# Moving the work around layer 1's attention: PSUM banks for its first chains, another DMA queue for its input, and a softmax sum on TensorE

## The chip, the core and the metric

The kernel runs on one core of one Trainium2 chip. A core has five engines that work beside one another and wait for each other through semaphores: TensorE (PE, matrix products, with its weight loads shown as PEld), VectorE (DVE), ScalarE (ACT), GpSimd (POOL) and SyncE (SP), which here only issues DMA transfers. TensorE writes its results into PSUM, which has eight banks of 128 x 512 f32; the other operands lie in SBUF. The metric is the device time of the program in microseconds, given as the median of several runs.

## What is computed

The input x is 4 x 1024 x 512 in f32. Two layers follow, each of the form

```
xn = layernorm(x)
x  = x + attention(xn) * silu(feed_forward(xn))
```

Layer 0 has a linear attention with decay and a feed-forward with ternary weights and an exact gelu. Layer 1, where the change lies, has softmax attention with 16 heads of width 32 and a rotation of half of each head (rope), and a gated feed-forward with integer weights:

```
q, k, v = xn @ wq.T, xn @ wk.T, xn @ wv.T        (16 heads of 32)
q, k    = rope(q), rope(k)
p       = softmax(q k^T / sqrt(32))
s       = (p v) @ wo.T
```

## The kernel before

The 4096 rows are 32 tiles of 128 (t), or 8 blocks of 512. Layer 0's attention comes first, then its feed-forward, then layer 1's attention, then its feed-forward. TensorE's order is the order of the program; the other engines' instructions are put in order by a planner ahead of the run, from its own costs, and each engine then works strictly in that order. An instruction marked `keep_in_program_order` may not be moved ahead of what the program issues before it on its engine; later ones may still pass it in the planning.

**The end of layer 0.** `gate` (L646) finishes one tile of x after layer 0: y = projection plus a correction (L658, reads PSUM), tanh on ScalarE (L660), two VectorE passes (L661, L662), the addition of the old x on POOL (L663), a store of the tile to DRAM as x1 through SP's queue (L664), and the tile's moments (L105, L108). The last block's four tiles (28 to 31) are finished while layer 1 starts.

**The start of layer 1's attention.** PSUM is now split into `ring` (three tiles of two banks), `acc1` (one bank) and `y` (one bank). `heads_in` (L884) makes k, q and v of four heads of one batch element as six chains of matmuls: k half 0, k half 1, q half 0, q half 1, v half 0, v half 1 (halves of the 1024 tokens). A k or q chain ends with `raw`, a ScalarE copy (L905); eight small transfers on SP (L909) that bring each row's rotation partner into `rr`; the product with the cosines on VectorE (L912, reads PSUM); the product with the sines and the sum on POOL (L913, L914). There is one `rr` tile for half 0 and one for half 1, so k and q of a half use it in turn, and two `raw` tiles. The first six chains run alone (L1077); `spread` (L979) gives them a bank of `ring` and `acc1` alternately.

`rr` and the tiles for the maxima (`m2`) are set to zero on VectorE (L847, L850).

**Late tiles.** The last four tiles of x1 weren't normalised in layer 0. `late` (L862) reads each back from DRAM through SP (L866) and normalises it on ScalarE (L869, kept in program order; one buffer for x, one for the result); two steps afterwards `late_turn` (L873) transposes it on TensorE into `acc1`. Steps 0, 4, 8, 12 load, steps 2, 6, 10, 14 transpose.

**The main loop** (L1084) runs over steps s. A unit is 512 queries of one batch element and one group of four heads: 32 units of 8 steps. In step s TensorE computes scores for the row maxima of unit s // 8 (`top`: sq in two ring tiles, reduced by VectorE, L1004), scores with keys on the partitions ten steps behind (`expo`: sk in two ring tiles, the maximum subtracted by L1033, then the exponential p on ScalarE, L1038), and p times v another step behind (`weigh`: y). After a unit's eight steps `turn_max` (L1006) transposes its maxima through `acc1`; ScalarE copies them (mf, mh) and VectorE makes mT (L1016), which L1033 needs. Between these, `advance` runs a piece of a chain of the next four heads, or of the output projection `wo`, in `acc1`.

The softmax denominators: POOL adds the eight p tiles of a unit into `part` (L1065, L1067), and one group of matmuls with ones (`total`, L940) sums over the partitions into z; `divide` (L945) takes reciprocals on VectorE and multiplies on POOL. Only for the last unit (31) TensorE sums the first four p itself (z_last). In the last ten steps, and for what belongs to them, VectorE does the additions in POOL's place. During the last twelve steps with sq, weights for the feed-forward are loaded and converted on VectorE (L783).

Of the kernel before, what the change touches and what calls it, by code (L numbers as in the profile page):

```python
# [16 lines left out]
ALU = mybir.AluOpType  # L17
# [3 lines left out]
B, N, D = 4, 1024, 512  # L21
# [6 lines left out]
NBLK = NT // BLK  # L28
# [7 lines left out]
def kernel(ctx, tc, ins, out):  # L36
    nc = tc.nc
# [21 lines left out]
    x1_t = x1.rearrange("(t p) d -> t p d", p=P)  # L59
# [486 lines left out]
    with ExitStack() as es:  # L546
# [99 lines left out]
        def gate(blk, i):  # L646

            t = blk * TPB + i
            mv = mvs[blk]

            last = blk == NBLK - 1 and i >= 2
            x = p2.tile([P, D], F32, tag="x" if last else "xr", name=f"x0r_{t}")
            nc.sync.dma_start(out=x, in_=x_t[t])
            s = p2.tile([P, D], F32, tag="xq" if last else "s", name=f"s0_{t}")
            nc.sync.dma_start(out=s, in_=s0_t[t])
            sc = mv[:, 3, i : i + 1]
            y = p2.tile([P, D], F32, tag="y", name=f"y0_{t}")
            nc.vector.scalar_tensor_tensor(y, rows, mv[:, 0, i : i + 1], ds.pop(i), ALU.mult, ALU.add)  # L658
            th = x1s[t] = p2.tile([P, D], F32, tag="th", name=f"th0_{t}", bufs=5)
            nc.scalar.activation(th, y, AF.Tanh, scale=sc)  # L660
            nc.vector.scalar_tensor_tensor(th, th, 1.0, y, ALU.add, ALU.mult)  # L661
            nc.vector.scalar_tensor_tensor(th, th, sc, s, ALU.mult, ALU.mult)  # L662
            nc.gpsimd.tensor_tensor(th, th, x, ALU.add)  # L663
            nc.sync.dma_start(out=x1_t[t], in_=th)  # L664
            moments(p2, th, st1[:, t, :], f"c{t}")

        def turn_out(blk, i):
# [139 lines left out]
    with ExitStack() as es:  # L807
# [6 lines left out]
        def ring(name):  # L814
            return pp.tile([P, 2, 512], F32, tag="ring", name=name, bufs=3)

        def acc1(name):
            return pp.tile([P, 512], F32, tag="acc1", name=name)

        TB = N // P  # L820
# [23 lines left out]
        partner = []  # L844
        for i in range(2):
            m2 = wp.tile([P, TPB, P], F32, tag=f"m2_{i}", name=f"m2_{i}")
            nc.vector.memset(m2, 0.0)  # L847
            twice.append(m2)
            rr = wp.tile([P, 512], F32, tag=f"rr_{i}", name=f"rr_{i}")
            nc.vector.memset(rr, 0.0)  # L850
            partner.append(rr)

        def cols4(out, lhsT, rhs, start, stop):
# [8 lines left out]
        def late(i):  # L862

            t = NTILE - TPB + i
            x = p2.tile([P, D], F32, tag="x", name=f"x1_{t}", bufs=1)
            nc.sync.dma_start(out=x, in_=x1_t[t])  # L866
            xn = p2.tile([P, D], F32, tag="xn", name=f"xn1_{t}", bufs=1)
            tc.keep_in_program_order(
                nc.scalar.activation(  # L869
                    xn, x, AF.Identity, bias=shift[:, t : t + 1], scale=st1[:, t, 1:2]  # L870
                )
            )
            return xn  # L873
# [131 lines left out]

        def turn_max(u):  # L1006

            tp = acc1(f"tr_m_{u}")
            for i in range(TPB):
                nc.tensor.transpose(tp[:, i * P : (i + 1) * P], twice[u % 2][:, i, :], ident)  # L1010
            mf = p2.tile([P, 512], F32, tag="mf", name=f"mf_{u}", bufs=1)
            nc.scalar.copy(mf, tp)
            mh = p2.tile([P, 512], F32R, tag="mh", name=f"mh_{u}", bufs=1)
            nc.scalar.copy(mh, mf)
            mTs[u] = p2.tile([P, 512], F32R, tag="mT", name=f"mT_{u}")
            nc.vector.scalar_tensor_tensor(  # L1016
                mTs[u], mh.bitcast(F32), second, mf, ALU.mult, ALU.add
            )
# [34 lines left out]
        def exps(e):  # L1053
            if not 0 <= e < TB * nu:
                return
            u, kb = divmod(e, TB)
            pT = pTs[e] = p2.tile([P, 4, 512], F32, tag="pT", name=f"pT_{e}", bufs=3)
            expo(u, kb, pT)


            k0 = TB // 2 if u == nu - 1 else 0
            add = nc.vector if e + LAG >= TB * nu else nc.gpsimd
            if kb == k0 + 1:
                parts[u] = p2.tile([P, 4, 512], F32, tag="part", name=f"part_{u}")
                add.tensor_tensor(parts[u], pTs[e - 1], pT, ALU.add)  # L1065
            elif kb > k0:
                add.tensor_tensor(parts[u], parts[u], pT, ALU.add)  # L1067
# [6 lines left out]
        nu, LAG = len(units), TB + 2  # L1074
        yTs = {b: {} for b in range(B)}
        chain = None
        for m, c in enumerate(heads_in(0, 0, spread)):  # L1077
            chain = c
            advance(8)
            if m == 3:  # L1080
                norm1(NBLK - 1, p2)
        must, spare = deque(), deque()
        mx, mTs, pTs, ys, parts, lates, soon = {}, {}, {}, {}, {}, {}, {}
        for s in range(TB * nu + LAG + 1):  # L1084

            e = s - LAG
            if s % (2 * TB) == 0 and s < TB * nu:  # L1090

                assert not must
                n = s // (2 * TB) + 1
                if n < 4 * B:
                    b, g = divmod(n, 4)
                    must.extend(heads_in(b, g, acc1))
                    if g == 3 and b + 1 < B:
                        load1(b + 1)
                left = 2
            if s in soon and s < TB * nu:  # L1100
                spare.extend(wo_out(*soon.pop(s), acc1))
            if s % 2 == 0:

                chain = None
                if spare and left and s < TB * nu:
                    chain = spare.popleft()
                    left -= 1
                elif must:
                    chain = must.popleft()
            if s == 2 * TB:  # L1110
                W["wo"] = shared_tile("wo", "wo")
                tc.keep_in_program_order(
                    nc.sync.dma_start(
                        out=W["wo"], in_=ins["woT"].rearrange("(k p) n -> p k n", p=P)
                    )
                )
            if s % 4 == 0 and s // 4 < TPB:
                lates[s + 2] = s // 4, late(s // 4)
            if s < TB * nu:
                u, j = divmod(s, TB)  # L1120
                if j == 0:
                    mx[u] = p2.tile([P, TPB, 4, 2], F32, tag="mx", name=f"mx_{u}")
                for pair in range(2):
                    top(u, j, pair, mx[u])
                if j == TB - 1:
                    m2 = twice[u % 2].rearrange("p q (h c) -> p q h c", c=HD)
                    for c in range(2):
                        nc.vector.tensor_reduce(m2[:, :, :, c], mx[u], AX.X, ALU.max, negate=True)
                    del mx[u]
            late_exp = s >= TB * nu  # L1130
            if late_exp:
                exps(e)
            if 1 <= e <= TB * nu:
                u, kb = divmod(e - 1, TB)
                if kb == 0:
                    ys[u] = pp.tile([P, 512], F32, tag="y", name=f"y_{u}")
                weigh(u, kb, pTs[e - 1], ys[u])
                if u == nu - 1:

                    if kb == 0:  # L1140
                        z_last = acc1("z_last")
                    if kb < TB // 2:
                        total(z_last, pTs[e - 1], kb, TB)
                pTs.pop(e - 2, None)
                if kb == TB - 1:
                    yr = p2.tile([P, 512], F32, tag="yr", name=f"yr_{u}", bufs=1)
                    nc.scalar.copy(yr, ys[u])
                    ys[u] = yr
            held = 0
            zu = (s - (6 if s >= TB * nu else 4)) // TB - 2  # L1150
            if s % TB == 0 and 0 < s <= TB * nu:
                turn_max(s // TB - 1)
            elif s % TB == (6 if s >= TB * nu else 4) and 0 <= zu < nu - 1:
                z = ring(f"z_{zu}")[:, 0, :] if s >= TB * nu else acc1(f"z_{zu}")
                total(z, parts.pop(zu), 0, 1)
                divide(units[zu], ys.pop(zu), z)
                b, g, qh = units[zu]
                if g == 3:
                    soon[s + 4] = b, qh, yTs[b]
            elif s in lates:  # L1160
                late_turn(*lates.pop(s))
            else:
                held = 1
                advance(1)
            if not late_exp:
                exps(e)
            advance(4 - held)
            if TB * nu - 12 <= s < TB * nu:

                nxt = weight(raw1, w0, True)  # L1170
                if loaded:
                    loaded()
                loaded = nxt
                if s == TB * nu - 1:
                    loaded()
# [310 lines left out]
```

## Time and profile before

| what | value |
|---|---|
| median of 3 runs | 3150.0 us (3148.52 to 3150.66) |
| the profiled execution | 3149.29 us, span 3147.5 us |
| TensorE busy | 3088.4 us, 98% |
| VectorE, ScalarE, POOL busy | 1905.1, 1196.1, 1501.4 us |
| mean granted TensorE clock | 0.994 |
| layer 0's last projection ends | about 1164.2 us |
| layer 1's first score matmul | 1198.15 us |
| layer 1's output projections start after the loop | about 2628.4 us |
| layer 1's feed-forward starts | 2657.81 us |

Times in the profile are microseconds from the start of the span; L909 is line 909 of the kernel. A line of the waits names who waited, for whom, the total, how often, and the longest. A line of the chain of waits gives the start, the length, the engine and the line. A line of the timeline gives the start, the length, the engine, the line and what it reads and writes; matmuls of one kind in succession are merged with their number. "SPq" is SP's DMA queue. Busy time of TensorE includes short stalls between pipelined matmuls, so a busy engine isn't always at full speed.

### The profile page before, as it was taken

What the parts mean: (1) busy time and instruction counts of PE and PEld (TensorE: products, weight loads), DVE (VectorE), ACT (ScalarE), POOL (GpSimd) and SP (SyncE); (2) the same over time, 40 slices, a digit from 0 to 9 for tenths busy, and PEclk for the clock granted to TensorE, in tenths of its full rate; (3) what the DMA queues carried; (4) which work ended last, traced back from release to release, by engine and by line L of the source; (5) the groups of instructions that cost most, each with busy time, mean ns of one, the idle gap of its engine ahead of it and who ended that gap; (6) DMA issues with size and microseconds to landing.
All of it is one profiled execution on the core that took longest, in us unless ns stands there. A gap on an engine that the chain in (4) does not pass through costs nothing.

```text
span 3147.5 us, 61092 instructions
## 1 busy us (share of the span) xinstructions
PE 3088.4 (98%) x26233; PEld 1765.4 (56%) x26233; DVE 1905.1 (61%) x2638; ACT 1196.1 (38%) x1696; POOL 1501.4 (48%) x615
## 2 busy tenths in 40 slices
PE   9999999999999998999999999999999999999998
PEld 5555555578777874443344444334444435888887
DVE  4444555468888775656656555555555684566655
ACT  3111111155555542444444444444444444333332
POOL 0000000034444344898888988888888970000001
PEclk9999999999999999999999999999999999999999
DMA  3111111122222231100001000010000013322211
GB/s 131 54 54 54 54 57 44 38 64 91 81 81 71 94 138 38 48 9 8 8 17 40 12 12 15 20 35 14 10 17 15 12 44 100 119 75 66 67 51 55
DMA packets 97799, 158.46 MB, mean 50 GB/s; under 512 B 13040, under 2 KB 26864, under 8 KB 97392
## 3 DMA queue, kind: packets, MB, share of 16 engines
q1 hardware_dynamic: 96704, 151.33, 15.5%
q8 instruction: 207, 3.39, 0.5%
q0 software_dynamic: 816, 3.15, 0.3%
q14 instruction: 72, 0.59, 0.1%
HBM read 104.10 MB, written 41.94 MB: 46 GB/s over the span
## 4 chain that ended last, share of the span: by engine, by line
PE 84%; DVE 11%; issue 2%; ACT 2%; POOL 1%; SPq 1%; DMA 0%; ACTq 0%; POOLq 0%; DVEq 0%
PE sk L1027 9%; PE sq L1000 8%; PE y L1046 8%; PE qk L350 7%; PE gate L1218 5%; PE up L1218 5%; PE dn L1240 5%; PE v1ps L856 4%; PE v0ps L324 3%; PE wo L333 3%; PE wo L856 3%; PE wq L856 3%; PE fc L588 3%; PE wk L856 3%; PE pj L641 3%; PE sk L1033 2%
## 5 line engine op out<-in xcount | busy, mean ns | idle before, releaser
L1067 POOL TENSOR_TENSOR part<-part,pT 128x2048 f32<-128x2048 f32 x184 | 844.8, 4591 | 25.7 <-ACT pT L1038 16.5
L1004 DVE TENSOR_REDUCE mx<-sq 128x2 f32<-128x1024 f32 x512 | 603.3, 1218 | 384.3 <-PE sq L1000 383.1
L1038 ACT ACTIVATE pT<-sk 128x1024 f32<-128x1024 f32 x512 | 496.3, 1021 | 619.4 <-PE sk L1033 616.1
L1027 PE MATMUL sk<-wqT,wkT 32*128 32x512 f32 x2048 | 332.5, 645 | 4.3 <-DVE mx L1004 4.3
L1000 PE MATMUL sq<-wkT,wqT 32*128 32x512 f32 x2048 | 322.5, 641 | 6.1 <-ACT pT L1038 5.1
L1046 PE MATMUL y<-pT,v 128*32 128x512 f32 x2048 | 276.3, 610 | 0.2 <-ACT pT L1038 0.2
L609 POOL TENSOR_TENSOR sums<-sums,h 128x512 f32<-128x512 f32 x112 | 162.9, 1455 | 228.9 <-ACT h L593 223.8
L641 PE MATMUL pj<-wpj,hp 128*128 128x512 f32 x1024 | 265.2, 397 | 5.8 <-DVE hp L601 4.9
L588 PE MATMUL fc<-xp,wfc 128*128 128x512 f32 x1024 | 261.1, 397 | 2.9 <-ACT h L593 2.0
L1262 POOL TENSOR_TENSOR th<-th,x 128x512 f32<-128x512 f32 x31 | 40.1, 1295 | 457.9 <-DVE th L1261 377.0
L1033 PE MATMUL sk<-mT,onesr 2*128 2x512 f32 x1024 | 239.3, 788 | 2.2 <-DVE mT L1016 2.2
L357 POOL TENSOR_TENSOR qd<-qT,wqkv 128x512 f32<-128x512 f32 x32 | 41.1, 1285 | 405.0 <-ACT qT L355 379.1
L350 PE MATMUL qk<-xnT,wqkv 128*128 128x512 f32 x512 | 230.0, 602 | 0.7 <-ACT xnT L148 0.7
L641 PEld LDWEIGHTS pj<-wpj,hp 128*128 128x128 f32 x1024 | 190.0, 188 | 58.2 <-DVE hp L601 17.4
L588 PEld LDWEIGHTS fc<-xp,wfc 128*128 128x128 f32 x1024 | 187.3, 188 | 44.4 <-ACT h L593 5.0
L1027 PEld LDWEIGHTS sk<-wqT,wkT 32*128 32x128 f32 x2048 | 99.9, 184 | 138.0 <-issue 111.4
L1218 PE MATMUL gate<-xp,wf 128*128 128x512 f32 x704 | 174.1, 389 | 0.0
L1065 POOL TENSOR_TENSOR part<-pT,pT 128x2048 f32<-128x2048 f32 x31 | 141.2, 4555 | 69.0 <-ACT pT L1038 68.8
L1218 PE MATMUL up<-xp,wf 128*128 128x512 f32 x704 | 173.8, 389 | 0.0
L1240 PE MATMUL dn<-wf,hp 128*128 128x512 f32 x704 | 173.5, 389 | 0.0
L601 DVE TENSOR_TENSOR hp<-h,hp 128x512 fp32r<-128x512 f32 x128 | 116.9, 913 | 76.2 <-ACT hp L598 76.1
L350 PEld LDWEIGHTS qk<-xnT,wqkv 128*128 128x128 f32 x512 | 95.2, 191 | 112.8 <-issue 104.2
(219 smaller groups left out, 4543.4 us busy)
## 6 DMA issues: line engine op xcount, KB each, us to landing
s<-s SPq DMA_DIRECT2D x96, 256.0 KB
x<-x SPq DMA_DIRECT2D x36, 256.0 KB
x<-in_x SPq DMA_DIRECT2D x32, 256.0 KB
raw_fc<-in_w_fcT SPq DMA_DIRECT2D x32, 256.0 KB
x0f<-in_x SPq DMA_DIRECT2D x32, 256.0 KB
x0r<-in_x SPq DMA_DIRECT2D x32, 256.0 KB
x<-th SPq DMA_DIRECT2D x32, 256.0 KB
xnT<-xnT_d SPq DMA_DIRECT2D x8, 1024.0 KB
```

The source lines that it names most:

```text
L350: nc.tensor.matmul(a, lhsT=wqkv[k][:, c0 : c0 + P], rhs=xnTs[blk][:, k, :], start=(k == 0), stop=(k == KD - 1),)
L588: nc.tensor.matmul(a, lhsT=wfc[k][:, c * P : (c + 1) * P], rhs=xp[n][:, k, :].bitcast(F32R), start=(k == 0 and n == 0), stop=(k == KD - 1 ...
L641: nc.tensor.matmul(ds[i], lhsT=hparts[blk, c][n][:, i * P : (i + 1) * P], rhs=wpj[c], start=(c == 0 and n == 0), stop=(c == NH0 - 1 and n ...
L856: nc.tensor.matmul(out[r0 : r0 + HD, :], lhsT=lhsT[:, r0 : r0 + HD], rhs=rhs, start=start, stop=stop,)
L1000: nc.tensor.matmul(sq[:, hh, :], lhsT=qT[r, q0 : q0 + P], rhs=kT[r, n * 512 : (n + 1) * 512], start=True, stop=True,)
L1004: nc.vector.tensor_reduce(mx[:, qt, 2 * pair : 2 * pair + 2, n], sq, AX.X, ALU.max)
L1027: nc.tensor.matmul(sks[h // 2][:, h % 2, :], lhsT=kT[r, kb * P : (kb + 1) * P], rhs=qT[r, qh * 512 : (qh + 1) * 512], start=True, stop=False,)
L1038: nc.scalar.activation(pT[:, 2 * pair : 2 * pair + 2, :], sks[pair], AF.Exp, scale=QKS)
L1046: nc.tensor.matmul(y[r, :], lhsT=v[:, kb, r], rhs=pT[:, h, :], start=(kb == 0), stop=(kb == TB - 1),)
L1067: add.tensor_tensor(parts[u], parts[u], pT, ALU.add)
L1218: nc.tensor.matmul(a, lhsT=ws[n, c][:, k, :], rhs=xp[m][:, k, :], start=(k == 0 and m == 0), stop=(k == KD - 1 and m == 1),)
L1240: nc.tensor.matmul(ds[i], lhsT=hparts[blk, c][n][:, i * P : (i + 1) * P], rhs=w, start=(c == 0 and n == 0), stop=(c == NH1 - 1 and n == 1),)
```

## The change

It has three parts.

1. In `gate`, for the last block only, the addition of x goes from POOL to VectorE and the store of x1 from SP's queue to POOL's. The four clearing passes of `m2` and `rr` go from VectorE to POOL. The loads in `late` are kept in program order.
2. The first six chains of layer 1 take the six banks of the three ring tiles, one each, in place of `spread`.
3. For unit 30 (`nu - 2`) the additions into `part` are left out, and `total` runs on each p tile as it comes, eight groups of matmuls into `acc1`. Its `divide` comes with its last y. Since `acc1` is taken meanwhile, unit 29's z and unit 31's transposed maxima go to a ring tile. Step 6 as the late time of z is gone.

```diff
-            nc.gpsimd.tensor_tensor(th, th, x, ALU.add)
-            nc.sync.dma_start(out=x1_t[t], in_=th)
+            add, queue = (nc.vector, nc.gpsimd) if blk == NBLK - 1 else (nc.gpsimd, nc.sync)
+            add.tensor_tensor(th, th, x, ALU.add)
+            queue.dma_start(out=x1_t[t], in_=th)
...
-            nc.vector.memset(m2, 0.0)
+            nc.gpsimd.memset(m2, 0.0)
...
-            nc.vector.memset(rr, 0.0)
+            nc.gpsimd.memset(rr, 0.0)
...
-            nc.sync.dma_start(out=x, in_=x1_t[t])
+            tc.keep_in_program_order(nc.sync.dma_start(out=x, in_=x1_t[t]))
...
-            tp = acc1(f"tr_m_{u}")
+            tp = ring(f"tr_m_{u}")[:, 0, :] if u == nu - 1 else acc1(f"tr_m_{u}")
...
+            if u == nu - 2:
+                return
...
-        for m, c in enumerate(heads_in(0, 0, spread)):
+        firsts = [ring(f"first_{i}") for i in range(3)]
+        firsts = [firsts[i][:, n, :] for i, n in ((0, 0), (0, 1), (1, 1), (1, 0), (2, 1), (2, 0))]
+        for m, c in enumerate(heads_in(0, 0, lambda name: firsts.pop(0))):
...
-                if u == nu - 1:
+                if u >= nu - 2:
                     if kb == 0:
-                        z_last = acc1("z_last")
-                    if kb < TB // 2:
+                        z_last = acc1(f"z_{u}")
+                    if u < nu - 1 or kb < TB // 2:
                         total(z_last, pTs[e - 1], kb, TB)
...
+                    if u == nu - 2:
+                        divide(units[u], ys.pop(u), z_last)
+                        soon[s] = units[u][0], units[u][2], yTs[B - 1]
...
-            zu = (s - (6 if s >= TB * nu else 4)) // TB - 2
+            zu = (s - 4) // TB - 2
...
-            elif s % TB == (6 if s >= TB * nu else 4) and 0 <= zu < nu - 1:
-                z = ring(f"z_{zu}")[:, 0, :] if s >= TB * nu else acc1(f"z_{zu}")
+            elif s % TB == 4 and 0 <= zu < nu - 2:
+                z = ring(f"z_{zu}")[:, 0, :] if zu == nu - 3 else acc1(f"z_{zu}")
```

## The prediction, made before the changed kernel was run

> **What bounds the kernel now.** I read the page first: TensorE against the other engines, and its clock.
>
> ```profile
> PE 3088.4 (98%) x26233; PEld 1765.4 (56%) x26233; DVE 1905.1 (61%) x2638; ACT 1196.1 (38%) x1696; POOL 1501.4 (48%) x615
> ...
> PEclk9999999999999999999999999999999999999999
> ```
>
> TensorE is busy for 98% of the span. Time can be won only where it waits (59 us of 3147.5), or where its clock is low, which tenths of forty slices hide. So the list of waits on PE comes next, and it points to the seam before layer 1 and to the end of its attention.
>
> ```profile
> PE v1ps L856 <- DVE wqT L912: 5.8, 1, 5.8
> ...
> PE wk L856 <- DVE y L658: 2.3, 1, 2.3
> PE sk L1033 <- DVE mT L1016: 2.2, 1, 2.2
> ```
>
> These are single waits. The first two, and one of 1.24 before chain 4, are for the one PSUM bank (acc1) that chains 2, 4 and 6 of the first six share. The chain of waits tells more: through the seam it runs over SP, not over a bank.
>
> ```profile
> 1174.94 1.29 POOL th L663
> 1177.16 0.81 SPq L909
> ...
> 1193.24 2.02 DMA rr<-raw_wq
> 1195.48 1.27 POOL rr L913
> 1196.83 1.28 POOL wqT L914
> 1198.15 1.01 PE sq L1000 x5
> ```
>
> The first score matmul (sq, 1198.15) waits for the rotated q: eight small partner copies each for k half 0, k half 1 and q half 0, 24 issues of about 0.67 us one after the other on SP, then a landing of 2 us and two POOL passes of 1.27. They begin at 1177.16 only because SP holds the four x1 stores and the first late load ahead of them; their data was there at 1171.24 (ScalarE's copy raw_wk, 1170.65 + 0.59). Last, the clock by stretches of time (columns: stretch, length, busy PE, PEld, DVE, ACT, POOL, granted clock, DMA share, GB/s):
>
> ```profile
> 1191.40:1194.00 2.60, 2.60 (x52) 2.40 (x56) 2.37 (x9) 0.00 (x0) 1.21 (x1) 0.50 0.18 35
> 1194.00:1198.00 4.00, 3.77 (x84) 3.27 (x76) 0.66 (x5) 0.15 (x1) 2.44 (x2) 0.63 0.13 24
> ...
> 2600.00:2603.00 3.00, 1.43 (x13) 0.36 (x14) 3.00 (x3) 0.84 (x1) 0.00 (x0) 1.00 0.00 0
> 2603.00:2606.00 3.00, 3.00 (x20) 1.62 (x20) 0.72 (x1) 2.20 (x4) 0.00 (x0) 0.54 0.00 0
> ```
>
> After the gap of 5.8 the clock is half; a 64-matmul chain that takes 3.66 us in the timeline takes 6.40. After the 2.24 us wait at 2601.57 it is half again.
>
> **The change, part 1: banks and SP queue.** With six banks the chains run back to back: 1164.10 + 6 x 3.65 = 1186.0, instead of ending at 1197.77. But the sq matmul does not follow the chains, it follows SP. From the first partner copy to sq took 1198.15 - 1177.16 = 21.0, and nothing in that stretch is changed. The x1 stores go to POOL, the first late load is pinned behind the copies, so the first copy follows raw_wk. Earliest: the first chain ends at 1167.76, plus a copy of 0.59 and a small hand-over, 1168.5. Latest: as now behind both tanh passes, 1171.3. On VectorE two memsets of 0.48 go and four adds come (0.69 each, as other two-input 128x512 rows there), while its 1.17 wait for POOL goes: y of the last tile moves little. I take the middle, 1170.0. Then sq starts at 1191.0, **7.15 earlier**. PE's gap is now in one piece, 1186.0 to 1191.0.
>
> Here a rule of the Trainium skill stands beside the row (TensorE: Matmul & The Clock Gate, Part 1: The HAM clock gate): an idle window of about 3.4 us halves the clock, a busy one brings it back. By the rule a 5 us gap may or may not contain a whole idle window, and costs half of one window, 1.7, or 0. By the rows, one half-busy stretch was enough (2.24 idle), and after a gap of 5.8 the clock was low from the restart at 1191.37 until about 1197 (0.63 over four us leaves 3 us low), 5.6 us at half speed, a loss of 2.8. The row decides: 2.8 of the 7.15 go again, since work after the restart keeps PE full. By the rule's good end the whole sum would be 3142.7, by the row 3145.5. **Seam: -4.35**, from -8.65 (first copy at 1168.5, no clock loss) to -3.0 (1171.3, with it).
>
> The stores on POOL: four issues; the three weight loads took 0.92, 0.76, 0.75 there. After the last add (about 1176) that leaves POOL free at 1177, before its first rotation (1170.0 + 7.4 = 1177.4). The rule against it (SBUF, State Buffer; Summary: rules for kernel authors) is that GpSimd-issued descriptors starve under some VectorE modes. If each slips by a VectorE instruction (0.69), the first rotation is 2.8 late; but the q rotation that sq needs is 11 us later, so nothing on the path. The four memsets on POOL lie in its idle time (11.0 before 1165.58); the nearest row, 0.205 for 128x128, gives about 0.8 each, between 0.2 and 1.3. One may wait for a buffer that VectorE frees as late as 1172.3, and the stores queue behind it; the second half's copies need it at about 1175.4.
>
> **Part 2: the pin on all four late loads.** The pin holds for i = 1, 2, 3 too. Now load 1 is issued at 1199.38, right after its buffer is free. Pinned, it stands behind the eight copies of the next k half 1, issued from 1212.52 to 1217.86, at the old times. Issue 1217.96, landing 2.0 (rr) to 2.44 (x0r), 2.4 taken: 1220.4; normalising 0.82: 1221.2; the transpose now starts at 1219.59. **+1.7.** Load 2 stands behind the copies that end at 1231.93: 1232.0 + 2.4 + 0.82 = 1235.25 against 1234.57, **+0.7**. Load 3 has no copies ahead of it. Load 0 has 3 us to spare. So +2.4, between 0 (if the copies fall later in the order) and 3.7 (if the q copy on ScalarE, 1218.22, queues behind the late normalising).
>
> **Part 3: PE sums the last unit but one.** Eight groups of eight matmuls, 0.9 each (z rows of the chain: 0.86 and 0.90), come in as p arrives; one group (2618.99) goes, and with it seven POOL or VectorE adds of 4.6 or 2.3. I price it by the distances between the starts of successive y groups, from 2567.70 to 2610.94 (the timeline of PE; these three are steps 7 to 9):
>
> ```profile
> 2596.97 1.06 PE L1046 MATMUL y<-pT,v 128*32 128x512 f32 x8
> ...
> 2602.00 1.07 PE L1046 MATMUL y<-pT,v 128*32 128x512 f32 x8
> ...
> 2605.67 1.94 PE L1046 MATMUL y<-pT,v 128*32 128x512 f32 x8
> ```
>
> Now they are 4.68, 5.45, 5.46, 5.90, 4.89, 2.89, 5.03, 3.67, 5.27, sum 43.2. An undisturbed early step is 4.6: sq, y, sk and one exponential in a ring, the new group in it as well, so 5.5. Steps 3 and 4 are long now because conversions (L783) last 3.6 and 2.4 beside POOL's adds against 0.41 alone; without the adds they are 5.5. In step 7 PE waited 2.24 for mT, which stood behind a 4.8 conversion and an add that both go; steps 8 and 9 ran at half clock. New: 5.5, 6.4 (with the other z), 5.5, 5.5, 5.3, 3.8, 3.2, 3.2, 3.2, sum 41.6: -1.6. The z group that went: -0.9. **Tail: -2.5**, between +5.4 (6.3 of net matmul, 0.9 regained) and -5 (low clock at 2541 to 2555 lifts too). Once mT is ready in time, what is late next is PE's own order.
>
> **The sum.** -4.35 + 2.4 - 2.5 = -4.45. The profiled execution took 3149.29 (span 3147.5, 1.8 around it), so it would take 3144.8; its distance to the median, 0.7, is noise, and from 3150.0 the forecast is **3145.5**. A difference of 0.2% (6.3 us) is about what a measurement tells from none.
>
> **Rivals.** (B) Full gain: first copy at 1168.5, PE's gap 3.5 and no low clock, late loads hidden: -8.65 - 2.5, 3138.9; with the low clock 3141.7. For it: the first chain has ended by 1167.76. Against: ScalarE now takes both tanh first. Chance 0.27.
> (C) Slower: the late loads hold ScalarE. It works in order; now it runs normalising 2 at 1226.42, ahead of the copy mf at 1228.02 that frees acc1 for v1ps. If that order stays while load 2 lands at 1234.4, mf waits 7.2, and at the step before 3.0; both gaps exceed the 2.24 that halved the clock, 2.8 each: 15.8 lost against 6.85 won, 3159. It decides for slower from 13.2 lost, so only if both waits fall on PE. Against: an order laid out anew may put mf first. Chance 0.13.
> (D) No effect in the tail: groups fully paid, mT still late, +5.4 with the seam's -4.35 and the loads' 2.4: 3153.5. For it: the score ring is tight, and z and the maxima now take slots of it. Chance 0.10.
> My forecast (A) has 0.50. About a fifth of A, and nearly all of B, is below 3143.7: faster 0.36. C, with a little of D, is above 3156.3: slower 0.14. The rest, 0.50, is within. The range runs from B's middle to D, with a tenth left out on each side: 3139 to 3154; A alone 3142 to 3149.
>
> **What would show it.** Right: first partner copy near 1170, chains back to back to 1186, one PE gap before sq and a clock of 0.5 after it; late transposes that wait for normalising; no wait of sk on mT; full clock from 2600 to 2610. Wrong: copies still late on SP, a chain waiting for a bank, mf behind a late load, or y steps over 6 us in the tail.

## The result, and the profile after

The changed kernel takes 3152.57 us in the median of 14 runs (3146.31 to 3156.58), the kernel before 3150.73 in the median of the 14 runs beside it (3146.23 to 3153.89). The ratio is 1.0005, with a 95% interval from 0.9997 to 1.0013: between 0.9 us faster and 4.1 us slower. The forecast of 3145.5 was 7 us too low, and the measured time lies inside its range; the outcome is "no change that can be measured". Behind it stand three parts: the forecast had them at -4.35 (the seam's first chains), +2.4 (the late loads) and -2.5 us (the tail), the profiles show 0.0, +6.7 and -2.7. Only the last was right.

The page of the profile after says little more than that TensorE still bounds the kernel.

```profile
span 3144.5 us, 61189 instructions
...
PE 3082.8 (98%) x26289; PEld 1762.9 (56%) x26289; DVE 1890.0 (60%) x2636; ACT 1196.0 (38%) x1696; POOL 1476.0 (47%) x614
```

This execution's span is 3.0 us shorter than that of before, although the median is longer: it is the fastest of the 14. So the span must not be read as the gain. I cut both executions at the same instructions of TensorE: **A** is from layer 1's first chain to the first sq, **B** from there to the first sk (step 10), **C** from there to the first y of unit 30, **D** from there to layer 1's feed-forward (`gate`). Where the granted clock is 0.5, the text speaks of half clock. The column "half clock in C" gives the time lost to it: each slice's length times (1 - granted clock), added up over slices of 5 or 10 us.

| | A | B | C | D | A + B | half clock in C |
|---|---|---|---|---|---|---|
| before | 34.05 | 37.01 | 1332.54 | 90.11 | 71.06 | 6.8 |
| after | 34.05 | 43.74 | 1325.74 | 87.43 | 77.79 | 0 |

The seam (A + B) lost 6.73 us, the tail (D) won 2.68. The 6.80 us won in C, where the change edits nothing, are 13 us at half clock (2541 to 2555) which this execution did not have; they are taken up below.

The list of waits on PE between 1160 and 1245 us shows what became of the seam. Its columns are: who waited for whom, us in total, times, longest.

```profile
PE first L859 <- DVE wkT L915: 8.3, 1, 8.3
PE tr_x_l L882 <- DVE wqT L915: 3.6, 1, 3.6
PE first L859 <- DVE wqT L915: 1.5, 1, 1.5
PE tr_x_l L882 <- ACT v L931: 1.4, 1, 1.4
...
PE first L859 <- ACT v L931: 0.7, 1, 0.7
```

(L859 is now the matmul of the chains, L915 the product with the cosines, L882 the late tile's transpose.) The wait of 5.8 before the sixth chain is gone (0.7 is left of it), and the second chain, which had waited 2.3, waits 8.3. Three of these waits are of the first six chains, `first`, which have a bank each. The timeline of PE has them one by one, with the wait and its releaser in brackets:

```profile
1163.71 3.66 PE L859 MATMUL first<-xnT,wk 128*32 128x256 f32 x64
1175.70 5.64 PE L859 MATMUL first<-xnT,wk 128*32 128x256 f32 x64 [8.32 <-DVE wkT L915]
1181.16 3.63 PE L859 MATMUL first<-xnT,wq 128*32 128x256 f32 x64
1186.27 3.66 PE L859 MATMUL first<-xnT,wq 128*32 128x256 f32 x64 [1.49 <-DVE wqT L915]
1189.75 3.68 PE L859 MATMUL first<-wv,xnT 128*32 128x128 f32 x128
1194.13 3.70 PE L859 MATMUL first<-wv,xnT 128*32 128x128 f32 x128 [0.70 <-ACT v L931]
1197.76 1.14 PE L1003 MATMUL sq<-wkT,wqT 32*128 32x512 f32 x8
```

Chains 2, 4 and 6 wait, and each is the second one placed in its two-bank tile: the order of banks in the diff is (0,0), (0,1), (1,1), (1,0), (2,1), (2,0). Each begins when the chain in the *other* bank of its tile has been read. Chain 1's bank was last read by VectorE at 1174.97 to 1175.64, behind all its work on the last tiles of layer 0, and chain 2 starts at 1175.70, at half clock (5.64 instead of 3.66).

On SP's queue the change did what it was to do (start, time for all, queue, line, number):

```profile
1170.79 16.91 SPq L912 DMA_DIRECT2D rr<-raw_wk  x16
1187.82 11.32 SPq L912 DMA_DIRECT2D rr<-raw_wq  x16
...
1212.13 5.34 SPq L912 DMA_DIRECT2D rr<-raw_wk  x8
1217.57 0.39 SPq L869 DMA_DIRECT2D x<-x  x1
```

The first copy went at 1170.79 instead of 1177.16. But 16 copies of wk now take 16.91 us, since chain 2's result came so late. The last line is late load 1, behind eight copies. Three stretches show the clock, in the columns of the prediction (granted clock third from the end):

```profile
1168.00:1176.00 8.00, 0.30 (x4) 0.20 (x8) 7.51 (x16) 1.92 (x3) 1.08 (x2) 0.59 0.35 120
1222.00:1228.00 6.00, 4.93 (x40) 2.41 (x44) 2.56 (x3) 0.59 (x1) 0.00 (x0) 0.54 0.14 27
2600.00:2610.00 10.00, 10.00 (x92) 2.93 (x88) 3.54 (x5) 7.25 (x10) 0.88 (x1) 1.00 0.00 0
```

The first is the wait of 8.32, the second follows the wait of the late transpose. The third answers to the tail's rows of before: full clock, and PE without a gap. The tail's y steps (timeline of PE):

```profile
2595.59 1.06 PE L1049 MATMUL y<-pT,v 128*32 128x512 f32 x8
...
2599.33 1.06 PE L1049 MATMUL y<-pT,v 128*32 128x512 f32 x8
2602.49 1.07 PE L1049 MATMUL y<-pT,v 128*32 128x512 f32 x8
2605.64 1.07 PE L1049 MATMUL y<-pT,v 128*32 128x512 f32 x8
2608.81 1.06 PE L1049 MATMUL y<-pT,v 128*32 128x512 f32 x8
```

The wait of 2.2 for mT is gone, and steps of 5.03, 3.67 and 5.27 have become 3.16, 3.15 and 3.17.

### The profile page after: what moved, and what is told of

Its sections match the earlier page's. It is cut to its first block, busy times and chain, and to the rows that moved or that the text cites. A ratio compares the mean times of both kernels' runs of the same rounds, so it can differ in the third digit from the quotient of the medians.

```text
span 3144.5 us, 61189 instructions
## 1 busy us (share of the span) xinstructions
PE 3082.8 (98%) x26289; PEld 1762.9 (56%) x26289; DVE 1890.0 (60%) x2636; ACT 1196.0 (38%) x1696; POOL 1476.0 (47%) x614
## 4 chain that ended last, share of the span: by engine, by line
PE 85%; DVE 10%; ACT 2%; issue 1%; DMA 1%; POOL 0%; SPq 0%; ACTq 0%; POOLq 0%; DVEq 0%
PE sk L1030 9%; PE sq L1003 8%; PE y L1049 8%; PE qk L350 7%; PE gate L1229 5%; PE up L1229 5%; PE dn L1251 5%; PE wq L859 4%; PE v0ps L324 3%; PE wo L333 3%; PE v1ps L859 3%; PE wo L859 3%; PE fc L588 3%; PE wk L859 3%; PE pj L641 3%; PE sk L1036 2%
## 5 line engine op out<-in xcount | busy, mean ns | idle before, releaser
L1072 POOL TENSOR_TENSOR part<-part,pT 128x2048 f32<-128x2048 f32 x180 | 826.7, 4593 | 19.7 <-ACT pT L1041 10.9
L1030 PE MATMUL sk<-wqT,wkT 32*128 32x512 f32 x2048 | 326.2, 639 | 3.7 <-DVE mx L1007 3.4
```

The source lines that it names most:

```text
L1030: nc.tensor.matmul(sks[h // 2][:, h % 2, :], lhsT=kT[r, kb * P : (kb + 1) * P], rhs=qT[r, qh * 512 : (qh + 1) * 512], start=True, stop=False,)
```

## The experiments

All runs side by side. A to D are each from one profiled execution; a ratio is that of the medians, with its 95% interval, to the runs of the kernel before on the same chip.

| | A | B | C (half clock in it) | D | A + B + D | ratio |
|---|---|---|---|---|---|---|
| before | 34.05 | 37.01 | 1332.54 (6.8) | 90.11 | 161.17 | |
| after | 34.05 | 43.74 | 1325.74 (0) | 87.43 | 165.22 | 1.0005 (0.9997 to 1.0013) |
| e1_order | 28.62 | 46.62 | 1330.71 (5.1) | 87.43 | 162.67 | 0.9996 (0.9987 to 1.0006) |
| e2_pin0 | 33.70 | 37.14 | 1330.36 (5.1) | 87.43 | 158.27 | 0.9996 (0.9985 to 1.0007) |
| e3_tail | 34.35 | 37.01 | 1333.22 (5.1) | 87.43 | 158.79 | 0.9995 (0.9985 to 1.0006) |
| e4_seam | 34.21 | 43.79 | 1325.92 (0) | 88.49 | 166.49 | 1.0013 (1.0005 to 1.0021) |
| e5_no_banks | 29.22 | 38.82 | 1330.76 (5.1) | 87.42 | 155.46 | one run |
| e9_queue | 28.05 | 38.63 | 1333.22 (5.2) | 90.00 | 156.68 | 0.9972 (0.996 to 0.9985) |
| e6_best | 28.69 | 39.62 | 1332.81 (6.8) | 87.42 | 155.73 | 0.9972 (0.9963 to 0.998) |
| e7_two_queues | 26.54 | 38.82 | 1330.98 (3.4) | 87.44 | 152.80 | 0.9965 (0.9953 to 0.9977) |
| e8_filled | 26.35 | 37.61 | 1337.81 (8.5) | 87.43 | 151.39 | 0.9958 (0.9943 to 0.9972) |
| before_again | 34.03 | 37.00 | 1326.78 (0) | 88.51 | 159.54 | one run |
| after_again | 34.41 | 43.77 | 1325.61 (0) | 87.43 | 165.61 | one run |

The medians of e1_order, e2_pin0 and e3_tail don't tell these kernels from before or from one another: what is said of them rests on the stages of one execution each. That the first two would be 6 us below the changed kernel, as expected, the medians don't show (about 3, with intervals that overlap).

### The order of the six banks

```diff
-        firsts = [firsts[i][:, n, :] for i, n in ((0, 0), (0, 1), (1, 1), (1, 0), (2, 1), (2, 0))]
+        firsts = [firsts[i][:, n, :] for i, n in ((0, 0), (1, 0), (2, 0), (0, 1), (1, 1), (2, 1))]
```

> The changed kernel, with the six first chains given the same six banks in another order: the first halves of the three ring tiles first, then the second halves. Stage A is the time from the start of the first chain to the first score matmul (34.05 us before and after the change), stage B from there to the first sk (37.0 before, 43.7 after). Theory 1, a chain in the second half of a ring tile waits until the first half's chain has been read: chain 2 starts at the end of chain 1, the wait of 8.3 us is gone, chain 4 waits about 1 us for the read of chain 1, and A falls to about 28 (the first partner copy 7.1 after chain 1's start, plus the 21.0 that SP and POOL take). Rival, the bank still holds layer 0's last projection, or VectorE is only too busy: whichever chain comes second or takes that bank waits until VectorE is through with the last tiles, and A stays at 34 or falls by less than 2. B stays at 43.7 in both. Whole time: 6 below the changed kernel by theory 1, the same by the rival.

A fell to 28.62. Timeline of PE in this run:

```profile
1165.21 7.11 PE L859 MATMUL first<-xnT,wk 128*32 128x256 f32 x128
1172.14 3.64 PE L859 MATMUL first<-xnT,wq 128*32 128x256 f32 x64
1177.18 3.66 PE L859 MATMUL first<-xnT,wq 128*32 128x256 f32 x64 [1.40 <-DVE wkT L915]
1180.66 7.17 PE L859 MATMUL first<-wv,xnT 128*32 128x128 f32 x256
1193.83 2.09 PE L1003 MATMUL sq<-wkT,wqT 32*128 32x512 f32 x8 [6.00 <-POOL wqT L917]
1195.85 3.64 PE L859 MATMUL wk<-xnT,wk 128*32 128x256 f32 x32
```

The first three chains run without a gap, and the one wait that is left is that of chain 4, again the second one in chain 1's tile. Chain 4 waits only 1.40 us for the bank for which chain 2 had waited 8.32, and chain 2, now in another tile, begins at once. So the wait goes with the tile, not with the bank. With the chains done at 1187.8, the first sq waits for the copies, as the prediction had it; the gap of 6.0 then costs half clock (2.09 for eight sq matmuls that take 1.14 elsewhere, 3.64 for a half chain that takes 1.93). Of the 5.4 us won in A, B gives 2.9 back (it had been expected to stay at 43.7).

### The pins on the late loads

```diff
-            tc.keep_in_program_order(nc.sync.dma_start(out=x, in_=x1_t[t]))
+            load = nc.sync.dma_start(out=x, in_=x1_t[t])
+            if i == 0:
+                tc.keep_in_program_order(load)
```

> The changed kernel with only the first of the four late loads kept in program order. If the pin on loads 1 and 2 makes the waits of 3.6 and 1.4 us at the late transposes, both go, with the low clock after the first, and stage B falls from 43.7 to 37 or 38; A stays at 34.05, the whole is about 6 below the changed kernel. Rival, the waits come from the x1 stores on POOL's queue, which land late: B stays at 43.7 and the whole time doesn't change.

B is 37.14, as before the change. No late transpose waits longer than 0.5 us, and the clock stays full at 1222. The three later pins cost 6.6 us. The kernel after shows how: load 1 (1217.57) lands so that ScalarE normalises it only at 1220.22, and the copy of a q chain stands behind it.

```profile
1220.22 0.81 ACT L872 ACTIVATE xn<-x,shift,st 128x512 f32<-128x512 f32 x1 [8.14 <-DMA x<-x]
1220.94 0.56 ACT L908 COPY raw_wq<-wq 128x512 f32<-128x512 f32 x1
```

That copy lets VectorE read the bank (`acc1`) which the transpose needs. So the transpose waits 3.6 us, not the 1.7 of the late data alone, and half clock follows. The second wait, 1.4 us for the copy `v`, has the same form: load 2's normalising starts at 1239.58, the copy behind it at 1240.30.

### The tail alone, and the seam without the tail

e3_tail is the kernel before with part 3 of the change only; e4_seam is the kernel after without part 3. The core of the edit, as e3_tail has it:

```diff
+            if u == nu - 2:
+                return
...
-                if u == nu - 1:
+                if u >= nu - 2:
...
+                    if u == nu - 2:
+                        divide(units[u], ys.pop(u), z_last)
```

> The kernel before with the third part alone, TensorE's sums for the last unit but one. Stage D is the time from that unit's first y to the start of layer 1's feed-forward (90.1 before, 87.4 after the change). Theory: D is 87.4, mT is no longer waited for and the clock stays full there; A 34.05 and B 37.0 as before; the whole about 2.7 below the kernel before. Rival, the gain in D came with the seam's new order or with a lucky clock: D is 90 or more (the net cost of the matmuls, 6.3, comes through, and D is up to 93 where the clock isn't low before either).

> The changed kernel without its third part: queue, banks and pins alone. By my account A is 34.05 (nothing won), B 43.7 (6.7 lost) and D 90.1: the whole is about 6.7 above the kernel before, where the low clock falls alike. Rival, the seam's parts cost nothing beyond the profiled execution's luck: the same as before.

D is 87.4 with part 3 whatever else is in the kernel, and 90.11, 90.00, 88.51 and 88.49 without it. By the granted clock half clock took 3.4, 6.8, 1.7 and 1.7 us of these four stretches. So part 3 is worth 1.1 to 2.7 us here, and the gain goes with half clock: all nine executions with part 3 have none in D, all four without it have some, though D isn't longer in proportion. e4_seam is slower than before by 1.6 to 6.6 us; its A + B + D is 5.3 above that of before (6.9 in A and B, less 1.6 in D, where 90.1 was expected).

### The queue and the banks apart

e9_queue is the kernel before with the new queue alone. e5_no_banks is e2_pin0 with `spread` for the first six chains in place of the six banks.

```diff
+            add, queue = (nc.vector, nc.gpsimd) if blk == NBLK - 1 else (nc.gpsimd, nc.sync)
+            add.tensor_tensor(th, th, x, ALU.add)
+            queue.dma_start(out=x1_t[t], in_=th)
...
+            nc.gpsimd.memset(m2, 0.0)
...
+            nc.gpsimd.memset(rr, 0.0)
```

> The kernel before with the queue's part alone: the last block's additions on VectorE, its stores on GpSimd's queue, the clears on GpSimd; no banks, no pinned loads, no change at the tail. The theory that this part alone makes the seam's gain: first chain to first score matmul 29.2 us (34.05 before), 38.8 us to step 10, 90.1 us from unit 30's first weighing to the gate; 3 us under the time before. Rival, that the pinned first load or the banks are needed for it: 33 us or more to the first score matmul, or a wait of 2 us or more for the first late tile.

```diff
-        firsts = [ring(f"first_{i}") for i in range(3)]
-        firsts = [firsts[i][:, n, :] for i, n in ((0, 0), (0, 1), (1, 1), (1, 0), (2, 1), (2, 0))]
-        for m, c in enumerate(heads_in(0, 0, lambda name: firsts.pop(0))):
+        for m, c in enumerate(heads_in(0, 0, spread)):
```

> The changed kernel with only the first late load pinned and the six first chains in alternating banks as before the change (SP's queue is free, GpSimd stores and clears). The theory that the six banks bring nothing as they are ordered: first chain to first score matmul within 1 us of the 33.70 of the same kernel with them. Rival, that the banks bring the early chains something and the order merely hides it: 36 us or more.

The queue's part alone takes A from 34.05 to 28.05 and the whole time down by 4.7 to 12.6 us (its stages show 4.5; where the rest lies is open). The additions, the stores and the clears moved together in it; what each is worth was not run apart. Without the banks, A is 29.22; with them (e2_pin0) 33.70, so neither the expectation (within 1 us) nor its rival (36 or more) came true. The six banks in their order cost 4.5 us in A (2.8 in A + B, since B is 1.7 longer without them, behind a gap of 4.14), and in the other order (e6_best below, A + B = 68.31) they stand where two alternating places do (68.04). The waits on PE in e9_queue say why the banks had nothing to win:

```profile
PE sq L1001 <- POOL wqT L915: 3.1, 1, 3.1
PE wk L857 <- DVE y L658: 2.2, 1, 2.2
PE v1ps L857 <- DVE wqT L913: 1.3, 1, 1.3
```

The wait of 5.8 before the sixth chain, which in the kernel before looked like one for a bank, is 1.3 here, with the same bank. That bank held the fourth chain, and in the kernel before ScalarE's copy for the fourth chain reads:

```profile
1190.00 0.59 ACT L905 COPY raw_wq<-wq 128x512 f32<-128x512 f32 x1 [3.79 <-DMA rr<-raw_wk]
```

VectorE could read the bank only behind this copy, and the copy waited for one of two `raw` tiles, that is for a partner copy on SP. In e9_queue the same copy runs at 1185.28, 4.7 us earlier, as the copies on SP do (1172.48 instead of 1177.16). The bank was held by the queue.

### What is left of the gap before sq

e6_best has the order of e1_order and the pin of e2_pin0. e7_two_queues adds a third `rr` (in storage that is idle then) and a second queue:

```diff
-                rr = partner[half]
+                rr = partner[2 if nm == "0_0" and n == "wq" and half == 0 else half]
...
-                        nc.sync.dma_start(
+                        queue = nc.scalar if nm == "0_0" and n == "wk" and half == 1 else nc.sync
+                        queue.dma_start(
```

e8_filled adds to that matmuls whose result is not used, in front of the main loop:

```diff
+        fill = ring("fill")[:, 0, :]
+        for i in range(TPB):
+            for k in range(KD):
+                cols4(
+                    fill[:, i * P : (i + 1) * P], xnTs[0][0][:, k, i * P : (i + 1) * P],
+                    W["wv"][:, k, :P], k == 0, k == KD - 1,
+                )
```

> The changed kernel with three edits: the six first chains take the first halves of the three bank pairs before the second halves, only the first late load keeps its place on SP, and the later two go where the scheduler puts them. The theory that each piece is worth what its stage showed: first chain to first score matmul about 28.6 us (34.05 before), first score matmul to the first score matmul of step 10 between 37 and 40 us (37.01 before; up to 2.9 of it half clock after the gap of 6 us in front of the score matmul), first weighing of unit 30 to the gate 87.4 us (90.11 before). In sum 5 to 8 us under the time before, a ratio of 0.9975 to 0.9985. Rival, that half clock returns what is won whatever the order of the work: 43 us or more between the two score matmuls, and a ratio within 0.9995 to 1.0005.

> As e6_best, and the partner copies of wk's second half are issued by ScalarE's queue, those of wq's first half go into a buffer of their own, so that they wait for no addition on GpSimd. The theory that the gap of 6 us in front of the first score matmul is 24 partner copies issued one after another on SP at 0.70 us each, and that half clock follows the gap: first chain to first score matmul about 24.5 to 26 us, PE's wait there 2 us or less, the score matmuls after it at full clock (8 in 1.1 us instead of 2.09), 37 us to step 10, and 3 to 6 us under e6_best. Rival, that copies from two queues land no sooner because they share the engines of the DMA: the wait in front of the score matmul stays at 5 us or more and the time is that of e6_best.

> As e7_two_queues, and behind the six first chains TensorE repeats the matmuls of one v chain (128 of 128x128, 3.58 us) into a bank that nobody reads, in the 3.92 us in which it waits for GpSimd. The theory that half clock follows the gap and nothing else: the score matmuls start where they did, 26.5 to 27 us behind the first chain, the half chain behind them takes 1.93 us instead of 3.62, 37.1 us to step 10 (38.82), and 1.7 us less in the whole. Rival, that the half clock there answers to something other than the gap (the load on the chip before it): the half chain stays at 3.4 us or more, and the time is that of e7_two_queues or above it.

e6_best did as expected in every stage; its ratio, 0.9963 to 0.998, is a little better than the stages, which show 5.4 us. In e7_two_queues A came to 26.54, not 24.5 to 26, and PE's wait to 3.92, not 2: ScalarE's copy `raw_wq` came only at 1178.76. ScalarE needed 6.74 us, until 1178.63, to issue its eight copies; but the profile names another cause, SP's copies out of the `raw` tile that this copy takes, and these had landed only just before (GpSimd works on them from 1178.56). Which of the two held it isn't separated. The sq matmuls ran at full clock as expected (1.14), but the half chain behind them did not, so that B is 38.82 and not 37. Timeline of PE in e7_two_queues:

```profile
1190.54 1.14 PE L1009 MATMUL sq<-wkT,wqT 32*128 32x512 f32 x8 [3.92 <-POOL wqT L923]
1191.61 3.62 PE L862 MATMUL wk<-xnT,wk 128*32 128x256 f32 x32
```

and in e8_filled:

```profile
1186.56 3.68 PE L862 MATMUL fill<-wv,xnT 128*32 128x128 f32 x128
1190.47 1.14 PE L1009 MATMUL sq<-wkT,wqT 32*128 32x512 f32 x8 [0.23 <-POOL wqT L923]
1191.54 1.93 PE L862 MATMUL wk<-xnT,wk 128*32 128x256 f32 x32
```

With the gap filled the sq matmuls start 26.35 us behind the first chain (26.54 without), and the half chain takes 1.93 instead of 3.62. This is half clock shown by itself, if in one execution of each: the work, its data and its start are the same, and only the idle time is gone. The executions with other gaps before sq agree: after 3.12 us (e9_queue), 4.14 (e5_no_banks), 6.00 (e1_order) and 6.07 (e6_best) half clock followed each time. B is 37.61 for 38.82; 0.5 of the 1.7 us went into a longer wait of the first late transpose (0.88 for 0.41). The median of e7_two_queues is 2.4 us below that of e6_best, where 3 to 6 were expected. The three intervals overlap, so that e7_two_queues beats e6_best, or e8_filled beats e7_two_queues, rests on the stages, not on the medians. All three are faster than before, by 0.2 to 0.6%, and their intervals lie below that of after, which was not run beside them; e8_filled has the lowest median, 3140.45 us (5 runs) beside 3153.71.

### Chance in the middle

Both kernels once more, not edited:

> The kernel before, not edited, in a second profiled execution. The theory of chance: between the first score matmul of step 10 and unit 30's first weighing it takes 1325.7 us and as much more as its phases of half clock cost (6.8 in the first execution, each phase 3.4), not the same phases as in the first; the seam repeats (34.0 and 37.0 us). Rival, that the phases belong to the kernel before: 1332.5 us and the same phases at the same places.

> The changed kernel, not edited, in a second profiled execution. The theory that its 1325.74 us from the first score matmul of step 10 to unit 30's first weighing (1332.54 before) were an execution without a phase of half clock there, which comes and goes from one execution to the next: this one has one or more such phases between 1240 and 2570 us and takes 1327.5 to 1333 us there, while the seam repeats to 0.5 us (34.0 and 43.7 us) and the tail to 0.2 us (87.4). Rival, that the change itself keeps half clock out of that stage: 1326 us again, and no slice of it under full clock.

The expectation for the kernel before held, to 1.1 us. The kernel ran C in 1326.78 us, without a phase of half clock; so the 1332.54 of its first execution don't belong to it. That for the kernel after failed: C took 1325.61, again without such a phase, while seam and tail repeated. One stretch of the same work, before first, before_again second:

```profile
2541.00:2554.00 13.00, 12.93 (x48) 3.62 (x44) 8.93 (x8) 3.52 (x4) 9.87 (x3) 0.53 0.14 40
```

```profile
2541.00:2554.00 13.00, 12.55 (x80) 4.33 (x76) 12.37 (x11) 7.02 (x8) 12.10 (x4) 1.00 0.20 57
```

Same kernel, same place, 0.53 and 1.00. Over all thirteen executions C follows the time lost: 1325.6 to 1326.8 where it is 0, 1331.0 at 3.4, 1330.4 to 1333.2 at 5.1 or 5.2, 1332.5 and 1332.8 at 6.8, 1337.8 at 8.5. So half clock explains the profile's "gain" of 6.8 us in C, if not all of every difference (1337.8 is 12 above for 8.5 lost). What remains open: the three executions with all the pins and the change's order of banks (after, after_again, e4_seam) had none in C, and neither had one of the two of the kernel before, while the nine others had some. Whether the late half clock at 1222 us shifts something that lasts to 2541, or three of three is chance, these runs can't tell. One thing speaks for chance: the profiled executions of after and e4_seam are the fastest of their 14 and 22 runs. That of e4_seam took 3146.32 us at a mean granted clock of 0.996, while the median is 3155.48 and 17 of the other 21 runs had 0.994 or less. So most runs of that kernel lost more to a low clock than the one with a profile; in which stage isn't recorded.

## Why the prediction was right and wrong

**"With six banks the chains run back to back."** This step failed. The chains waited 8.32 + 1.49 + 0.70, because a chain in the second half of a two-bank tile waits for the reading of the first half; with that order corrected (e1_order) they ran with one wait of 1.40. The step was read out of the list of waits, where `acc1` seemed to be the scarce thing. It was SP's queue. (The row of 6.40 us that the prediction sets beside a 64-matmul chain of 3.66 is a v chain of 128 matmuls, which takes 3.68 elsewhere; the factor is about the same.)

**"From the first partner copy to sq took 21.0, and nothing in that stretch is changed."** Right for the copies themselves: 21.0 in e9_queue (1172.48 to 1193.46) and 21.6 in e1_order (1172.27 to 1193.83). The first copy went at 1170.79, predicted 1170.0, but that start is 7.08 us behind the first chain's where 5.9 was predicted: close to the latest case that the prediction named (7.2). And in the changed kernel the path went over the chains: sq at 1197.76, predicted 1191.0. Measured for A was 0.0, in place of -7.15.

**Seam -4.35.** e9_queue measures the queue's part alone at -4.4 for A + B. The agreement is luck, since two errors cancel: before sq it won 6.0 where 7.15 was forecast (the first copy goes 7.07 us behind the first chain there, too), and the half clock behind the gap cost 1.6 where 2.8 was forecast. The 1.7 that the prediction takes from the rule is about what gaps of 3.1 to 4.1 us cost (1.6 to 1.8 in B of e9_queue, e7_two_queues and e5_no_banks); the 2.8 of its row fits gaps of 6 us (2.6 in e6_best, 2.9 in e1_order). And where it says that 2.24 us of idle time were enough for half clock, the same trace has chain 2 at full clock after 2.29 (1170.05, 3.66 us long). In the changed kernel the banks' order took the whole gain away.

**Late loads +2.4.** Too small: +6.6 in B (after against e2_pin0). (The first of its sums, 1221.2 against 1219.59, gives 1.6 and not 1.7, which changes nothing.) The step followed the late data to the transpose and stopped there. It named the other case, the q copy queued behind the late normalising, as the upper end, 3.7, and left out that a wait of 3.6 is long enough for half clock. Both happened: 3.6 and 1.4 of waits, and 6 us at a clock of 0.54.

**Tail -2.5.** Right: -2.68, with the nine distances as predicted (41.57 us where 41.6 was forecast). It is worth 1.1 where the execution without it had less half clock (before_again, e4_seam).

**The rivals.** (C), the slower one, put the late loads' harm at the copy mf. That did not occur (no wait for mf above 0.7), but its mechanism, work of ScalarE queued behind a late normalising, did, at `raw_wq` and `v`. (B) failed with the chains, and its idea that a gap of 3.5 leaves the clock full did not hold in the one gap below that length: 3.12 before sq in e9_queue was followed by half clock (eight sq in 2.09 us). (D), no effect in the tail, did not occur. Of the stores on GpSimd's queue no harm is seen: in the changed kernel they were issued in 0.54 to 0.58 us each, from 1166.57 to 1174.94, ahead of its first rotation at 1177.99.

**The sum.** 0.0 + 6.7 - 2.7 = +4.0 where -4.45 was predicted, the upper end of what the runs show (-0.9 to +4.1). That the measured time lies in the range is luck: the range reached up to (D), which did not occur, and two of its three steps were wrong.

## What to carry to other kernels

A wait for a bank names the bank's last reader; ask what the reader itself waited for before more banks are given, since here freeing the queue shortened the wait from 5.8 to 1.3 with the same bank. In this kernel, banks that are halves of one tile are waited for together: put consecutive pieces of work into different tiles. A pin that makes sure a load is late enough in one place holds in all places of the loop, so price it at each, with the engine that works in order behind it. And compare two executions stage by stage, with the granted clock of each: here the profiled execution of a kernel that was no faster was 3 us shorter.

## What the runs showed of the hardware

How long an idle stretch has to be for half clock isn't fixed. In e5_no_banks and e9_queue the second chain waits the same 2.17 us for the same thing:

```profile
1170.81 5.35 PE L859 MATMUL wk<-xnT,wk 128*32 128x256 f32 x64 [2.17 <-DVE y L658]
```

```profile
1171.24 3.66 PE L857 MATMUL wk<-xnT,wk 128*32 128x256 f32 x64 [2.17 <-DVE y L658]
```

It ran at half clock in one and at full clock in the other. The kernel before did both in its two executions: 3.66 us after a wait of 2.29, and 5.35 after one of 2.28 in before_again. The Trainium skill (TensorE: Matmul & The Clock Gate, Part 1: The HAM clock gate) says that the clock follows a free-running window of about 3.4 us, so that the same kernel may meet it at another phase; the losses in C and D, 1.7, 3.4, 5.1, 6.8 and 8.5 us, are multiples of half of such a window. The page has the clock halved after an idle window of that length. Here the measurement decides: 2.17 us sufficed, and in the middle of layer 1 half clock came where no wait of PE was longer than 0.9 us.

The granted clock also shows in the spread of one kernel. Of the 14 runs of the kernel after, the fastest (3146.31) has a mean granted clock of 0.996, and the three slowest (3155.19 to 3156.58) have 0.993. A clock lower by 0.003 over 3150 us makes 9.5 us, and they lie 8.9 to 10.3 apart. But two more runs at 0.996 took 3150.91 and 3152.65, so the clock, which is given to three places, doesn't account for the whole spread.

ScalarE took 6.74 us to issue eight small copies (0.84 each, e7_two_queues); SP took 5.83 for eight in the same run (0.73). ScalarE ran nothing else from 1171.89 to 1178.63: that was the price of the second queue here.
